# Layer 0's last two strips in a written order, the sums over A dealt anew between diffusion and sort, and X W gathered ahead of later rows of A^T

## The chip, the core and the metric

The kernel runs on one core of a Trainium2 chip. Its engines work side by side, each through its own list of instructions in order, and wait for one another by semaphores: PE (TensorE, matmuls into PSUM), DVE (VectorE), ACT (ScalarE), POOL (GpSimd) and SP (SyncE, which here only issues DMAs). POOL and ACT issue DMAs too. The metric is the device time of one execution in microseconds (us); lower is better.

## What is computed

Two layers over a graph of N = 2708 nodes with D = 128 features. `adj` is a 0/1 matrix; in the text A is `adj`, and A^T its transpose, which the kernel is also given. Cut to what matters, the reference is:

```python
# layer 0
deg = clip(adj.sum(axis=1), 1.0); dis = deg ** -0.5
diffusion = dis[:, None] * adj * dis[None, :] @ x - x
attn = softmax(beta * sim * adj, axis=1)            # sim: cosines of the rows of x
x = layernorm(x + diffusion + sigmoid(alpha) * (attn @ x - x))
# layer 1
XW = x @ W
s_col, s_row = XW @ a[0, :f], XW @ a[0, f:]
den = exp(leaky_relu(s_row[:, None] + s_col[None, :], 0.01))
num = A @ den
H = A @ (where(num != 0, den / num, 0) @ XW)
out = layernorm(x + H)
```

`den` has one of two forms for a pair of nodes, according to the sign of `s_row + s_col`. The kernel uses that: it sorts the nodes k by `s_row` and the nodes j by `s_col` into NG = 24 groups of at most 126, and gets `num` for one group of columns j from the one before by adding the rows of A^T whose k changes sides. So `num` needs one matmul of 128 rows per group and strip instead of a full product with A.

## The kernel before

The columns of A^T are cut into NS = 6 strips: five of 512 and a last one of 148. The rows are cut into NB = 22 blocks of 128. The work goes in these stages:

1. Attention of layer 0, strip after strip (to about 217 us).
2. **Diffusion** (L762 to L871 of the profile's lines). For each strip `s`, 22 matmuls (L771) add `x_sb` times the strip of A^T, which SP loads ahead (`load_strip`, L754). Then the strip is turned into rows (`to_rows`), attention is added (`h`), the layernorm's statistics are taken, `x1` is written and turned back (`x1_t`). Two matmuls give the scores of layer 1 as rows, `sb_ps`, for `s_row` (k = 1) and `s_col` (k = 0). `tally` counts on DVE how many of them lie beyond 256 thresholds, `picked` takes the same scores as a column, ACT copies `sr_b`, and `e2` is an Exp of the limited scores that POOL spreads into `e2_w`. At last X W (`xw`) is stored to HBM. Strips 0 to 4 are free for the scheduler to weave into one another; `strict` is filled at the last strip, and from there on `mm`, `dve`, `act` and `gps` keep the order in which the source writes them.
3. **Sums over A.** Group 0 starts from the sum of all rows of A^T weighted with `e2`. It is collected in `tot` by two kinds of job. An "e" (`first_strips`) loads the first 1536 columns of one row block (768 KB) into one of three `nat` buffers and adds them with 4 matmuls. A "k" (`kept_strips`) adds the row block's columns of strips 3 to 5, which are still in SBUF, with 6 matmuls. `fill("ek")` puts such jobs into PE's order at that place. Row blocks 0 to 7 (`EARLY_ROWS = 8`) are loaded by POOL and added in the diffusion, four behind strip 3 and four behind strip 4. The others are loaded by SP, each as soon as its buffer is free.
4. **Sort.** From the counts (`ct`, summed over all six strips) DVE and PE find the groups' bounds: `spread_ps`, `more` and `fits`, `reach_ps` and `can_ps`, then `ends`, a chain of eleven dependent DVE steps, `ends_ps`, `thr_ps`, `thr`. With them it numbers the nodes of k and of j (`k_gt` to `k_onp`, the same for j), and matmuls make tables of node numbers and scores (`tab_ps`, `k_sel`, `j_sel`). `k_no` and `j_no` are the node numbers by which POOL gathers rows of A^T (`gather`, into a ring of RING = 4) and rows of X W (`gather_xw`).
5. **Groups.** For each group g, `multiply` makes `num` strip by strip (three PSUM banks), DVE or ACT copies it to `q`, `carry` hands the first two rows on into the next group's ring buffer, ACT takes Ln, DVE divides, ACT takes Exp, and two groups later `weigh` adds `m_acc` from `q` and the gathered `xws`. The group's weights `wt` come from `gb`, an Exp of the group's scores; for groups 0 to 3 they are made on the spot, and for the later ones `g_r` is stored to `g_d` and read back, spread over all partitions.
6. H = A^T-blocks times `m_sb`, the last layernorm, and the output.

In stage 5 the helpers record most instructions under L176, those of stage 2 under L185, L190 and L195, so an instruction is found by its tile's name.

Of the kernel before, what the change touches and what calls it, by code (L numbers as in the profile page):

```python
# [11 lines left out]
ALU = mybir.AluOpType  # L12
# [25 lines left out]
EARLY_ROWS = 8  # L38
# [7 lines left out]
def grouped(  # L46
# [162 lines left out]
    def to_rows(acc, v, nb, ps):  # L209

        t = lp.tile([P, SW], F32, tag="to_rows", name="tr_sb", bufs=2)
        if v < nb * P:
            nc.gpsimd.memset(t[:, v : nb * P], 0.0)
        nc.scalar.copy(t[:, :v], acc[:, :v])
        rows = ps.tile([P, SW // P, P], F32, tag="tp", name="tr_ps")
        for b in range(nb):
            mm(nc.tensor.transpose, rows[:, b, :], t[:, ts(b, P)], ident)
        return rows

    def layernorm_stats(h, nb):  # L220
# [7 lines left out]
        nc.scalar.activation(rstd[:, :nb], mv[:, :nb, 1], AF.Sqrt, bias=eps)  # L228
# [61 lines left out]
    with ExitStack() as es:  # L290
# [173 lines left out]
        def attended(s, acc, total):  # L464
# [10 lines left out]
            rows = to_rows(acc, v, nb, ps_tp)  # L475
# [180 lines left out]
    def tally(s, src, lim, op, k):  # L656

        for h in range(2):
# [105 lines left out]
    for s in range(NS):  # L764
        v, nb = width(s), blocks(s)
        if 2 <= s + 1 < NS - 1:
            load_strip(s + 1)
        st = strips[s]
        acc = ps_acc.tile([P, SW], F32, tag="acc", name="dif_acc")
        for jb in range(NB):  # L770
            nc.tensor.matmul(  # L771
                acc[:, :v],
                x_sb[:, jb, :],
                st[:, jb, :v],
                start=(jb == 0),
                stop=(jb == NB - 1),
            )
        if s == 0:
            attended(*ended)
        if s == NS - 1:  # L780
            strict.append(s)
        rows = to_rows(acc, v, nb, ps_tp)

        h = work2.tile([P, SW // P, D], F32, tag="h", name="h")
        for b in range(nb):
            ib = s * 4 + b
            dve(
                "scalar_tensor_tensor", h[:, b, :], rows[:, b, :], dis[:, ib : ib + 1], att[:, ib, :],
                ALU.mult, ALU.add,
            )  # L790
        mv, rstd = layernorm_stats(h, nb)
        for b in range(nb):
# [3 lines left out]
        wide = nb * P  # L796
        if strict:
            fill("ekeke")
        tp = ps_tp.tile([P, SW // P, P], F32, tag="tp", name="x1_ps")
        for b in range(nb):  # L800
            mm(nc.tensor.transpose, tp[:, b, :], x1[:, s * 4 + b, :], ident)
        x1_t = work2.tile([P, SW], F32, tag="x1_t", name="x1_t")
        dve(
            "tensor_copy", x1_t[:, :wide], tp[:, :nb, :].rearrange("p b i -> p (b i)")
        )
        if strict:
            fill("e")

        cols = slice(s * SW, s * SW + wide)
        pbs = []  # L810
        for k, lim, op in ((1, ntheta, ALU.is_ge), (0, theta, ALU.is_le)):
            pb = ps_mm.tile([P, SW], F32, tag="mm", name="sb_ps")
            mm(
                nc.tensor.matmul, pb[:, :wide], wa_bc[:, k, :], x1_t[:, :wide],
                start=True, stop=True,
            )
            tally(s, pb, lim, op, k)
            pbs.append(pb)
        if strict:

            dve("tensor_reduce", ct, cnt.rearrange("p s k h -> p (k h) s"), AX.X, ALU.add)
            fill("ek")
            ct_ps = spread_out(ct, 4)
            far = small.tile([P, 2], F32, tag="far", name="far")
            dve("tensor_scalar", far, ct[:, 2:4], G + 0.5, None, ALU.add)
            fill("ek")
        nc.scalar.activation(sr_b[:, cols], pbs[0][:, :wide], AF.Copy, scale=1.0 - LEAK)
        for pb, dst in zip(pbs, (sr_p, sc_p)):
            for b in range(nb):
                ib = s * 4 + b  # L830
                junk = work2.tile([P, P], F32, tag="picked", name="picked", bufs=2)
                dve(
                    "scalar_tensor_tensor", junk, pb[:, ts(b, P)], 1.0, ident, ALU.mult,
                    ALU.mult, accum_out=dst[:, ib : ib + 1],
                )
        mine = slice(s * 4, s * 4 + nb)
        dve("tensor_scalar", low[:, mine], sr_p[:, mine], LIMIT, -LIMIT, ALU.min, ALU.max)
        if s == NS - 1:
            mine = slice((s - 1) * 4, s * 4 + nb)
        if s != NS - 2:  # L840
            nc.scalar.activation(e2_p[:, mine], low[:, mine], AF.Exp, scale=LEAK)
            nc.gpsimd.tensor_copy(e2_w[:, mine, 1], e2_p[:, mine])
        if strict:
            reach_ps, can = reached(ct_ps)
        pn = ps_mm.tile([P, SW // P, D], F32, tag="mm", name="xw_ps")
        for b in range(nb):
# [4 lines left out]
        xw = (nat if strict else work2).tile(  # L851
            [P, 2 if strict else 4, D], F32, tag="xw_last" if strict else "xw", name="xw",
            bufs=1 if strict else 2,
        )
        if strict:
            act(
                "activation", reach_b[64:], can[64:], AF.Copy, scale=-1.0,
                bias=Q + 1.0,
            )
            dve("tensor_copy", reach_b[:64], reach_ps[:64, :Q])  # L860
# [962 lines left out]
```

## Time and profile before

| | us |
|---|---|
| three runs | 750.27, 749.93, 749.05 (median 749.93) |
| the profiled execution | 753.27 |
| its span, first to last instruction | 751.5 |
| PE busy | 717.0 (95%) |
| DVE, ACT, POOL busy | 444.8, 418.6, 232.1 |
| mean granted PE clock | 0.972 |

| stretch of the span | us | PE busy | DVE busy | ACT busy | PE clock | DMA share |
|---|---|---|---|---|---|---|
| 336.0 to 347.9 | 11.90 | 10.21 | 4.92 | 0.90 | 1.00 | 0.74 |
| 347.9 to 361.0 | 13.10 | 9.95 | 7.92 | 2.45 | 0.90 | 0.76 |
| 361.0 to 375.5 | 14.50 | 11.07 | 8.48 | 0.76 | 0.85 | 0.87 |
| 375.5 to 388.0 | 12.50 | 9.35 | 10.47 | 8.25 | 0.73 | 0.41 |
| 435.6 to 444.5 | 8.90 | 8.90 | 8.19 | 6.71 | 1.00 | 0.76 |

A line of the timeline gives the start, the length, the engine, the source line, the operation, the tile written and the tile read, how many records were merged (a matmul in f32 leaves two records), and in brackets how long the engine had been idle and whose work it had waited for. The clock is the share of full TensorE speed that was granted.

### The profile page before, as it was taken

The page shows a single profiled execution, that of the slowest core. Times are in us where ns is not written, and L with a number is a line of the kernel's source. Part 1 is how long each engine was busy: PE and PEld are TensorE (multiplying, and loading weights), DVE is VectorE, ACT ScalarE, POOL GpSimd, SP SyncE. Part 2 cuts the span into 40 slices and gives each one's busy share as a digit, 9 for nine tenths or more (in the row PEclk, how much of TensorE's full clock was granted, in tenths as well). Part 3 has the DMA queues.
Part 4 walks back from the last instruction along what each step waited for, and adds up shares of the span by engine and source line. Part 5 has one row for each costly group of instructions (what it writes and reads, how often), then busy time and mean ns, then how long its engine had stood idle before and what let it go on. Part 6 is the DMA issues. An engine that isn't in the chain of part 4 may idle for free. (4 is left out here: it accounts for less than half of the span.)

```text
span 751.5 us, 7960 instructions
## 1 busy us (share of the span) xinstructions
PE 717.0 (95%) x2639; PEld 361.8 (48%) x2639; DVE 444.8 (59%) x927; ACT 418.6 (56%) x600; POOL 232.1 (31%) x239
## 2 busy tenths in 40 slices
PE   8999999999999999998789699999999999999995
PEld 5454444555564444445456244444444446444444
DVE  5677857576442345335585789999899993103032
ACT  4757777788741212110165889999999995001000
POOL 5867688879770000100003232222222300000000
PEclk9999999999989999999868899999999999999998
DMA  8868999989899999417837974444444531999970
GB/s 288 292 228 299 310 323 341 341 305 314 279 391 390 374 333 321 169 32 245 304 94 233 217 212 158 152 152 154 162 170 171 171 116 52 302 297 314 318 227 23
DMA packets 67524, 179.89 MB, mean 239 GB/s; under 512 B 4239, under 2 KB 18355, under 8 KB 64451
## 3 DMA queue, kind: packets, MB, share of 16 engines
q1 hardware_dynamic: 55012, 134.11, 52.0%
q0 software_dynamic: 6192, 42.29, 17.5%
q10 hardware_dynamic: 6270, 2.90, 1.3%
q8 instruction: 23, 0.38, 0.2%
q14 instruction: 27, 0.21, 0.1%
HBM read 176.44 MB, written 2.84 MB: 239 GB/s over the span
## 5 line engine op out<-in xcount | busy, mean ns | idle before, releaser
L201 POOL TENSOR_TENSOR total<-total,p_t 128x512 f32<-128x512 f32 (+3 forms) x111 | 125.4, 1131 | 36.1 <-ACT p_t L195 30.4
L176 PE MATMUL m_acc<-q,xws 128*128 128x512 f32 x240 | 123.0, 600 | 3.0 <-ACT q L176 3.0
L771 PE MATMUL dif_acc<-strip,x_sb 128*128 128x512 f32 (+1 forms) x264 | 104.0, 543 | 0.0
L176 PE MATMUL num<-ring,wt 128*128 128x512 f32 x216 | 98.4, 548 | 3.4 <-DVE q L176 1.8
L190 DVE SCALAR_TENSOR_TENSOR p_t<-sim,gentle,piece 128x512 f32<-128x512 f32 (+1 forms) x111 | 72.1, 670 | 48.2 <-PE sim L185 38.1
L185 PE MATMUL att_acc<-p_t,x_sb 128*128 128x512 f32 (+1 forms) x228 | 96.5, 549 | 2.5 <-ACT p_t L195 2.3
L176 DVE COPY q<-num 128x512 f32<-128x512 f32 (+1 forms) x141 | 83.9, 613 | 11.5 <-PE num L176 11.1
L176 DVE SCALAR_TENSOR_TENSOR q<-sr_b,nc_s,q 128x1536 f32<-128x1536 f32 (+1 forms) x48 | 77.8, 1623 | 16.1 <-ACT q L176 16.1
L195 ACT ACTIVATE p_t<-p_t,shift 128x512 f32<-128x512 f32 (+1 forms) x111 | 68.9, 654 | 30.9 <-DVE p_t L190 27.1
L176 PEld LDWEIGHTS m_acc<-q,xws 128*128 128x128 f32 x240 | 45.9, 192 | 60.3 <-issue 56.3
L1360 PE MATMUL h_acc<-ring,m_sb 128*128 128x512 f32 x164 | 72.3, 593 | 0.0
L176 ACT ACTIVATE q<-q,head,rest 128x1536 f32<-128x1536 f32 (+1 forms) x48 | 70.3, 1508 | 1.9 <-DVE ring L176 1.6
L771 PEld LDWEIGHTS dif_acc<-strip,x_sb 128*128 128x128 f32 x264 | 46.4, 190 | 48.4 <-issue 48.1
L176 ACT ACT_TABLE_LOAD x50 | 64.2, 1283 | 3.8 <-issue 2.9
L176 ACT ACTIVATE q<-q,c_s 128x1536 f32<-128x1536 f32 (+1 forms) x48 | 62.9, 1355 | 3.3 <-DVE q L176 3.0
L176 ACT ACTIVATE row<-row 128x1354 f32<-128x1354 f32 x44 | 58.2, 1323 | 11.0 <-DMA row<-in_adj 11.0
L176 PEld LDWEIGHTS num<-ring,wt 128*128 128x128 f32 x216 | 39.4, 192 | 48.4 <-issue 34.4
L185 PEld LDWEIGHTS att_acc<-p_t,x_sb 128*128 128x128 f32 x228 | 40.1, 198 | 45.4 <-ACT p_t L195 25.3
L1370 ACT COPY ht<-h_acc 128x512 f32<-128x512 f32 (+1 forms) x6 | 3.2, 535 | 91.6 <-PE h_acc L1360 91.5
L1375 DVE TENSOR_TENSOR hh<-rows,x 128x512 f32<-128x512 f32 (+1 forms) x6 | 3.8, 641 | 84.4 <-PE rows L1294 82.0
L176 POOL DMA_INDIRECT ring<-in_adj_t,k_no x18 | 19.5, 1082 | 107.9 <-PE num L176 100.3
L1360 PEld LDWEIGHTS h_acc<-ring,m_sb 128*128 128x128 f32 x164 | 30.8, 190 | 36.8 <-issue 36.8
(282 smaller groups left out, 910.9 us busy)
## 6 DMA issues: line engine op xcount, KB each, us to landing
row<-in_adj SPq DMA_DIRECT2D x44, 677.0 KB, 5.5
strip<-in_adj_t SPq DMA_DIRECT2D x10, 2816.0 KB, 15.6
piece<-in_adj_t SPq DMA_DIRECT2D x24, 1024.0 KB, 7.1
ring<-in_adj_t SPq DMA_DIRECT2D x20, 1024.0 KB, 5.1
nat<-in_adj_t SPq DMA_DIRECT2D x14, 768.0 KB, 6.3
x_sb<-in_adj_t SPq DMA_DIRECT2D x7, 1024.0 KB, 5.6
nat<-in_adj_t POOLq DMA_DIRECT2D x8, 768.0 KB, 6.3
piece<-in_adj_t SPq DMA_DIRECT2D x7, 512.0 KB, 7.5
```

The lines of the kernel that those rows point to most:

```text
L176: latest[engine] = op(*args, **kwargs)
L185: op(*args, **kwargs)
L190: return getattr(nc.vector, op)(*args, **kwargs)
L195: return getattr(nc.scalar, op)(*args, **kwargs)
L201: getattr(nc.gpsimd, op)(*args, **kwargs)
L771: nc.tensor.matmul(acc[:, :v], x_sb[:, jb, :], st[:, jb, :v], start=(jb == 0), stop=(jb == NB - 1),)
L1360: nc.tensor.matmul(acc[:, : h1 - h0], m_sb[:, kb + b, :], a[:, b, h0:h1], start=(kb + b == 0), stop=(kb + b == NB - 1),)
L1370: nc.scalar.copy(ht[:, h0:h1], acc[:, : h1 - h0])
L1375: nc.vector.tensor_tensor(hh[:, b0 : b0 + n, :], rows[:, :n, :], x1[:, ib + b0 : ib + b0 + n, :], ALU.add)
```

## The change

- `EARLY_ROWS` goes from 8 to 9. The early rows of A are issued after strips 1, 2 and 3, three each, and not after strips 3 and 4, four each.
- The loop body of the diffusion is cut into functions, and the loop runs over strips 0 to 3 only. Strips 4 (`s`) and 5 (`t`) are written out below it in one order, with `strict` filled right after the diffusion matmuls of strip 4. Those of strip 5 are dealt out in three parts (blocks 0 to 3, 4 to 17, 18 to 21) between the steps of strip 4.
- Score banks of strip 5 come from other PSUM pools. `picked` of strips 4 and 5 moves behind the counts, as does the Exp of `e2`, and X W of both strips is stored by one DMA.
- The `fill` jobs are dealt anew: fewer ahead of `ends_ps`, one between `ends_ps` and `thr_ps`, more behind `thr_ps`, fewer at the tables of j.
- In the sort, `valued_by_dve("j", 0, ...)` moves behind `rows_of_table("k", ...)`, twelve instead of five values of j are made ahead of the copy of the second table of k, and DVE instead of ACT copies `j_t[:, 0]`.
- The gathers go in the order `gather(1)`, `gather_xw(0)`, `gather(2)`, `gather_xw(1)`, `gather(3)`; before, `gather(1)` to `gather(3)` came ahead of both of `gather_xw`.
- The copies out of `tot` (`carry_in`) are split anew between ACT and DVE, two of them on ACT.
- The weights of groups 1 to 3 and `g_r` move from ahead of the first group to behind its second strip (`later_weights`, with one PSUM bank `c_ps`), and the read of `g_d` is cut in two DMAs, groups 4 to 7 first.
- `helped`, the copies of `num` that ACT makes, loses (1, 0), which DVE makes now.

```diff
-EARLY_ROWS = 8
+EARLY_ROWS = 9
...
+    for s in range(NS - 2):
+        v, nb = width(s), blocks(s)
+        if s > 0:
+            load_strip(s + 1)
+        acc = ps_acc.tile([P, SW], F32, tag="acc", name="dif_acc")
+        diffuse(s, acc)
...
+        for kb in {1: (0, 1, 2), 2: (3, 4, 5), 3: (6, 7, 8)}.get(s, ()):
+            first_strips(kb, nc.gpsimd)
...
+    s, t = NS - 2, NS - 1
+    acc = ps_acc.tile([P, SW], F32, tag="acc", name="dif_acc")
+    diffuse(s, acc)
+    strict.append("end of the diffusion")
+    acc_t = ps_acc.tile([P, SW], F32, tag="acc", name="dif_acc")
+    diffuse(t, acc_t, 0, 4)
+    h_s = mixed(s, turned(to_sbuf(acc, SW, 4), 4, ps_tp))
+    diffuse(t, acc_t, 4, 18)
+    mv_s = moments(h_s, 4)
+    to_x1(s, h_s, *mv_s)
+    tp = x1_turned(s)
+    diffuse(t, acc_t, 18, NB)
+    x1_s = x1_in_sbuf(s, tp)
+    row_s = scores(s, x1_s, 1, score_bank())
+    rows = turned(to_sbuf(acc_t, width(t), blocks(t)), blocks(t), ps_tp)
+    col_s = scores(s, x1_s, 0, score_bank())
+    tally(s, row_s, 1, (0,))
+    h_t = mixed(t, rows)
+    mv_t = moments(h_t, blocks(t))
+    shared_row(s, row_s)
+    fill("eke")
+    tally(s, row_s, 1, (1,))
+    to_x1(t, h_t, *mv_t)
+    tp = x1_turned(t)
+    tally(s, col_s, 0, (0,))
+    x1_t = x1_in_sbuf(t, tp)
+    fill("k")
+    row_t = scores(t, x1_t, 1, ps_tp.tile([P, SW], F32, tag="tp", name="sb_ps"))
+    col_t = scores(t, x1_t, 0, ps_acc.tile([P, SW], F32, tag="acc", name="sb_ps"))
+    tally(s, col_s, 0, (1,))
+    tally(t, row_t, 1)
+    tally(t, col_t, 0)
+
+    dve("tensor_reduce", ct, cnt.rearrange("p s k h -> p (k h) s"), AX.X, ALU.add)
+    fill("ek")
+    ct_ps = spread_out(ct, 4)
...
+    shared_row(t, row_t)
+    picked(t, col_t, sc_p)
+    picked(t, row_t, sr_p)
+    picked(s, row_s, sr_p)
+    fill("ek")
+    reach_ps, can = reached(ct_ps)
+    limited(s * 4, NB)
+    picked(s, col_s, sc_p)
+    act("activation", reach_b[64:], can[64:], AF.Copy, scale=-1.0, bias=Q + 1.0)
+    dve("tensor_copy", reach_b[:64], reach_ps[:64, :Q])
+    e2(s * 4, NB)
...
+    store_xw(s, xw, 6)
+    fill("ekekek")
...
+    fill("k")
     for h in range(2):
         hit = tmp.tile([P, NG - 1], F32, tag=f"hit{h}", name="hit")
...
-    fill("ekk")
+    fill("ekekk")
...
-    fill("ekekkk")
+    fill("kekekekek")
     j_gt = beyond("j", vj)
...
-    k_tab = table("k", k_onp, 0, *banks("x"), P - G, lambda: fill("e"))
+    k_tab = table("k", k_onp, 0, *banks("x"), P - G, lambda: fill("kk"))
     valued("k", 1, k_hot, low, 17)
+    valued("j", 1, j_hot, cs_p, 0, 12)
     j_run, j_ahead, j_of = numbered("j", j_hot)
+    k_no = rows_of_table("k", k_tab, G)
+    valued_by_dve("j", 0, j_hot, from_n)
+    k_tab = table("k", k_onp, 1, *banks("x"), 0, lambda: fill("kkk"))
+    valued("j", 1, j_hot, cs_p, 12)
     fill("k")
-    valued_by_dve("j", 0, j_hot, from_n)
-    k_no = rows_of_table("k", k_tab, G)
-    valued("j", 1, j_hot, cs_p, 0, 5)
-    k_tab = table("k", k_onp, 1, *banks("x"), 0, lambda: fill("kkk"))
-    valued("j", 1, j_hot, cs_p, 5)
-    fill("kkkk")
...
-    for g in range(1, RING):
-        gather(g)
+    gather(1)
...
+    dve("tensor_copy", j_t[:, 0, :], j_of_value[1])
...
+    weights(0, gb[:, 0, :])
+    j_tab = selected("j", j_t, [0, 1])
+    carry_in(0, (2, 3), by_dve)
...
+    j_no = rows_of_table("j", j_tab, P)
...
+    carry_in(1, (0, 1), by_act)
+    carry_in(1, (2, 3), by_dve)
...
-    for g in range(2):
-        gather_xw(g)
+    gather_xw(0)
+    gather(2)
+    gather_xw(1)
+    gather(3)
+
+    def later_weights():
+
+        o = ps_num.tile([P, SW], F32, tag="num", name="c_ps")
+        for g in range(1, 4):
+            spread_c(o[:, ts(g - 1, P)], g)
...
+        act("activation", g_r[:NG], o[:NG, 3 * P :], AF.Exp)
+        nc.sync.dma_start(g_d, g_r[:NG, P - G :])
...
+        for g in range(1, 4):
+            weights(g, gb[:, g, :])
+        for g0, g1 in ((4, 8), (8, NG)):
+            nc.sync.dma_start(
+                wt[:, g0:g1, P - G :],
+                g_d[g0:g1, :].unsqueeze(0).to_broadcast([P, g1 - g0, G]),
+            )
...
-    helped = {(0, 1), (0, 3), (1, 0)}
+    helped = {(0, 1), (0, 3)}
...
                 multiply(g, *item)
+                if (g, s) == (0, 1):
+                    later_weights()
```

`diffuse`, `to_sbuf`, `turned`, `mixed`, `moments`, `to_x1`, `x1_turned`, `x1_in_sbuf`, `scores`, `picked`, `shared_row`, `limited`, `e2` and `store_xw` hold the instructions of the old loop body. `moments` ends with ACT's square root, and `to_x1` begins with the reciprocal. `spread_c(o, g)` is the one matmul that lays the scores of group g over all partitions.

## The prediction

> **What bounds the kernel now.** I read the page's row of slices first, then windows by stage, then each engine in order of time between 336 and 445 us. All times below are us into the profiled span of the kernel before.
>
> ```profile
> PE   8999999999999999998789699999999999999995
> PEclk9999999999989999999868899999999999999998
> ```
>
> ```profile
> 388.00:405.90 17.90, 16.59 (x301) 13.71 (x301) 13.07 (x23) 10.60 (x45) 5.12 (x5) 0.81 0.43 148
> 405.90:435.60 29.70, 23.33 (x46) 9.75 (x47) 18.94 (x23) 22.74 (x23) 5.90 (x6) 0.83 1.01 222
> 444.50:640.00 195.50, 194.82 (x532) 93.40 (x531) 169.34 (x211) 184.87 (x169) 40.94 (x38) 1.00 0.43 148
> ```
>
> The columns are length, busy time of PE, PEld, DVE, ACT and POOL, then granted clock, DMA share and GB/s. From 444.5 on PE is busy 194.82 of 195.50 us: what starts earlier ends earlier by as much. The change acts ahead of that, where PE has holes and half clock. The holes, engine by engine:
>
> ```profile
> 357.23 0.20 DVE L176 TENSOR_REDUCE ct<-cnt 128x4 f32<-128x24 f32 x1
> 358.62 1.51 PE L176 MATMUL tot<-nat,e_w 128*32 128x384 f32 x8 [2.28 <-DMA nat<-in_adj_t]
> 361.03 1.53 PE L176 MATMUL spread_ps<-ident,ct 128*128 128x128 f32 x8
> 373.14 1.51 PE L176 MATMUL tot<-nat,e_w 128*32 128x384 f32 x8 [3.43 <-DMA nat<-in_adj_t]
> 375.56 0.62 PE L176 MATMUL ends_ps<-both,ones 128*128 128x23 f32 x2
> 388.03 1.53 PE L176 MATMUL tab_ps<-k_onp,k_ons 128*32 128x128 f32 x42 [2.49 <-DVE k_onp L176]
> 405.88 6.51 PE L176 MATMUL num<-x_sb,wt 128*128 128x512 f32 x12 [0.24 <-ACT gb L176]
> 425.11 2.05 PE L176 MATMUL m_acc<-q,xws 128*128 128x512 f32 x2 [3.00 <-ACT q L176]
> ```
>
> The chain is DVE's: counts `ct`, bounds, thresholds, places. Twice its next PE step (`spread_ps`, `ends_ps`) stands in PE's queue behind a sum over a row of A^T (an "e") that is still landing: `ct` is ready at 357.4, `spread_ps` runs at 361.03; `both` ends at 372.2, `ends_ps` runs at 375.56. That is 3.6 + 3.3 us.
>
> The last line names ACT, but ACT's power of that `q` had ended at 420.5. The DMA view, asked for the one issue at 405.14, gives the real releaser:
>
> ```profile
> xws<-xw_d,j_no POOLq DMA_INDIRECT x1, 19.8
> ```
>
> 405.14 + 19.8 = 424.9. The three gathers of A^T ahead of it on POOL's queue (400.19, 401.59, 402.95) landed after 9.4, 14.7 and 21.0 us: one queue, one behind the other.
>
> **The change, part by part.**
>
> *Sums inside the diffusion.* Nine e rows instead of eight, three each in strips 2, 3, 4 (before: 0-3 in strip 4's, 4-7 in strip 5's). Three rows cost PE 0.80 + 2.05 = 2.85 us (332.90 to 333.70 and 334.29 to 336.34). A strip without rows takes 22.7 (two tr_ps, 260.94 and 283.60). Strip 4's diffusion so ends at 260.1 + 3 x 22.7 + 3 x 2.85 = 336.8, not 332.9: 3.9 later. Against it, PE's 1.69 us wait for row 7 at 341.32 goes, and rows 9-11 can load from SP as soon as 6-8 are summed (about 314), long before their use at 346.
>
> The rule that speaks against this: the Trainium skill, "DMA: Bandwidth & Descriptors", Issuing engines are not separate DMA queues, says that DMAs of all issuers share the same 16 engines and interleave. POOL's rows 3-8 now fly beside the loads of strips 3 and 4, which landed 12.5 and 13.4 us after issue without such company. By the rule strip and three rows (5.77 + 2.36 MB at the 372 GB/s of 240 to 264) finish after 21.9 us; the strip is wanted 25.5 us after issue. Both give a loss of 0, the rule with a margin of 3.6.
>
> *Last two strips in written order.* From 336.8: four blocks of strip 5 (0.275 each) hide ACT's copy, tr_ps 337.9, `h` 338.6 to 339.7, four stats pairs in strict order (0.41 each, as at 352.06) to 341.35, rstd, x1 to 343.04; 14 blocks of strip 5 hide that, x_ps to 343.25, last four blocks to 344.35. Scores of strip 4 then; DVE: tally 345.4, `h` and stats of strip 5 to 347.4. The second tally waits for ACT's read of the same bank, which is queued behind rstd: 348.4, a new wait of 1.0. x1 to 349.75, tally, x1_t to 350.84, tally, four short tallies (0.293 each) from 351.6: `ct` at 352.9 instead of 357.23, **4.3 earlier**.
>
> *From ct to the k tables.* `spread_ps` at 353.1, no DMA ahead of it (row 11 is there). Eight of the twelve `picked` (0.21 each) now stand before `more`: 354.9, and `fits` end at 356.85. ACT writes reach_b at 357.9 (1.02 behind, as before) and only then loads the Exp table (1.28) for e2; before, that load lay in a wait at 357.11. DVE's `back` needs e2 and stands ahead of `ends`: 359.9 instead of 358.05, a new loss of 1.85. `ends` to `both` takes 6.5: `ends_ps` at 366.45 instead of 375.56, 9.1 earlier. One k between (1.1 at half clock) costs 0.2: `thr` 368.8 instead of 377.73. `k_of` ends 3.5 on, 372.3, and DVE has j_gt until 373.1.
>
> PE has "ekekk" before `ahead`, and it sat idle from about 362.4 to 366.4. Row: after the 3.43 us hole at 373.14 the clock stayed at 0.50 until 382, and e and k took 1.28 and 1.09 instead of 0.66. Five would end at 374.4, k_run at 375.0. Rule (the Trainium skill, "TensorE: Matmul & The Clock Gate", Part 1: The HAM clock gate): full clock returns after about 3.4 us of busy PE; then k_run waits for DVE alone, 373.1. The nearest row is the restart at 358.62, sums back to back as here: clock 1.00 from 362 on, 3.4 us later. I take half clock to 371: `ahead` at 372.9, k_run 373.5 instead of 381.94. k_onp takes the same 6.1: 379.6.
>
> Then "kekekekek" (5 k, 4 e). With three buffers row 21 is issued when row 18 is summed, 374.5. Such loads landed after 4.2 and 6.1 (issues at 341 and 352). At 5.0: 379.5, and e and k behind it end at 380.8, later than DVE. **k tables at 380.8 instead of 388.03: 7.2 earlier** (bounds: 379.6 and 383).
>
> *From the k tables to the first group (T = 380.8).* PE has been busy, so its clock should be full here, where before it read 0.50. k_no T+2.9 (was 3.6), then valued_by_dve (1.08), which before lay in the wait for k_no: j_run T+4.1, j_onp T+6.95 to T+10.1 (was T+10.95), j tables to T+11.35 (was T+14.4, because "kkkk" held PE). Twelve values of j now stand on ACT ahead of the copy of k table 1 (T+6.0, was T+7.8), where nothing waits. gb exp and weights(0) end 1.32 after the tables, T+12.7. Before, the first `num` came 2.2 us behind weights(0), since its bank waited for ACT's exps of groups 1 to 3; those are moved into group 0. gather(0) is issued at T+3.4 and took 7.0: hidden. **First num at 393.5 instead of 405.88; 5.2 of it here.**
>
> *First groups.* Moving the exps and three weights behind `num` (0,1) holds ACT's copy of (0,3) and delays the first Ln by 1.1 (S+8.4 from the first num S; was S+7.33). Dropping ACT's copy (1,0), which waited behind Ln and held PE 1.54, gives that back. X W of group 0 is issued at T+13.3 behind one gather alone and lands near S+6; `m_acc` wants it at S+16.4. Its cost: ring2 and ring3 are issued later, land near S+11 and S+18, wanted at S+15.5 and S+24. The half of weights' DMA for groups 4-7 comes first and is wanted at S+29. With PE no longer held at 425.11 nor cold to 430, what ends last is DVE's copies: step 3 starts at S+24.4 instead of S+29.76 (435.64). **5.3 earlier.**
>
> Sum: 7.2 + 5.2 + 5.3 = 17.7; I take 17, as some hand-overs have no row. The profiled execution took 753.27 (span 751.5); it would take about 736.3. The runs shown have a median of 749.93, 3.3 lower, so **732.9**.
>
> **Rivals.**
> B, the carry chain sets the start of the groups: each group's first two rows come from the one before through PE, DVE and back. If DVE, not X W, was last there, 5.3 goes: gain 12.4, 737.5. For it: DVE busy 18.94 of 29.70, ring copies between. Against: PE stood still at 425.11 after DVE had caught up at 423.1.
> C, PE becomes the bound before the k tables: half clock throughout and late rows put T at 386, and cold j tables take 2 more: gain about 8, 741.9. For it: clock 0.73 to 0.85 in those stages. Against: e and k fill DVE's time, and DVE was 10.47 of 12.50 busy.
> D, slower: the three-buffer ring. Rows 12, 15, 18, 21 each start when the row three before is summed, a loop of landing + 0.7. With landing L: row 21 at 347 + 4L + 2. At L = 4 to 6.3 it hides. At L = 12.1 (the longest seen) row 21 lands at 397.4, T is 398.7, 10.7 late, which eats the 10.5 gained behind it; from L = 12.1 on it decides, and L = 13 gives 753.7. Against: the 12.1 is one of 22 loads, median 6.3.
> That the written order isn't there is excluded: the built program's order shows it.
>
> **How the numbers follow.** A (as worked, 12.5 to 21.1) 0.66, B 0.15, C 0.12, D 0.05, other 0.02. A measurement tells 0.2%, 1.5 us. Best end: row 21 in time (1.2), k_run at 373.1 (0.4), the first two `num` at full clock (1.75): 21.1, 728.8. High end: C, 741.5. Faster 0.92, same 0.02, slower 0.06.
>
> **What would show it.** `ct` near 353, `spread_ps` directly behind it, `ends_ps` near 366, k tables near 381, first `num` near 393.5, no wait of `m_acc` 0 in group 2, PE full from about 410. Wrong if e rows 12 to 21 still wait for DMA, if the half clock covers 366 to 396, or if ring2 or ring3 lands late.

## The result, and the profile after

| | before | after |
|---|---|---|
| runs, median (lowest to highest) | 748.80 us (744.82 to 753.98, 20 runs) | **742.07 us** (736.38 to 748.73, 20 runs) |
| the profiled execution: time, span, mean granted clock | 753.27, 751.5, 0.972 | 739.68, 737.9, 0.982 |

The ratio is 0.9897, with a 95% interval of 0.9873 to 0.9920: 7.7 us faster (6.0 to 9.5). This ratio, like every ratio, interval and mean below, leaves out the runs that lie more than 1.5% above the fastest of their kernel (here the one of 748.73), which the medians and ranges contain. Forecast were 17 us, 732.9, with a range up to 741.5. The two profiled executions, set side by side, differ by 13.6 us, nearly twice as much as the runs. That gap between the pair of profiles and the runs is what the experiments had to explain.

First the profile after: its rows of PE's busy share and clock, then its windows from `ct` to the k tables, to the first `num`, to step 4, and the steady groups (columns: length, busy time of PE, PEld, DVE, ACT and POOL, clock, DMA share, GB/s).

```profile
PE   7999999999999999999798899999999999999995
PEclk9999999999979999999989999999999999999999
```

```profile
353.10:380.90 27.80, 22.57 (x285) 15.47 (x280) 22.27 (x79) 11.99 (x44) 0.93 (x5) 0.88 0.73 247
380.90:395.30 14.40, 12.49 (x267) 11.13 (x258) 10.25 (x17) 8.76 (x36) 3.76 (x2) 0.88 0.53 182
395.30:429.30 34.00, 30.68 (x76) 13.89 (x77) 29.33 (x40) 28.51 (x30) 12.63 (x10) 0.95 0.95 222
429.30:640.00 210.70, 208.92 (x568) 100.19 (x567) 170.98 (x224) 186.77 (x171) 41.79 (x38) 1.00 0.49 162
```

The stretch from the k tables to the first `num` has shrunk from 17.9 to 14.4 us, and PE is as full in the steady groups as it was (208.92 of 210.70). In time order, PE and DVE of the same trace:

```profile
353.13 0.20 DVE L176 TENSOR_REDUCE ct<-cnt 128x4 f32<-128x24 f32 x1
360.00 0.18 DVE L176 TENSOR_TENSOR back<-live,e_p 128x22 f32<-128x22 f32 x1 [1.52 <-ACT e_p L176]
366.65 0.59 PE L176 MATMUL ends_ps<-both,ones 128*128 128x23 f32 x2 [3.71 <-DVE both L176]
379.73 0.85 PE L176 MATMUL tot<-nat,e_w 128*32 128x384 f32 x8 [0.97 <-DMA nat<-in_adj_t]
380.89 1.38 PE L176 MATMUL tab_ps<-k_onp,k_ons 128*32 128x128 f32 x42
389.54 4.48 PE L176 MATMUL tab_ps<-j_onp,j_ons 128*32 128x128 f32 x88 [1.59 <-DVE j_onp L176]
395.32 1.99 PE L176 MATMUL num<-x_sb,wt 128*128 128x512 f32 x4 [0.29 <-ACT wt L176]
411.25 1.92 PE L176 MATMUL m_acc<-q,xws 128*128 128x512 f32 x2
```

`ct`, `ends_ps` and the k tables stand where the prediction had them (352.9, 366.45, 380.8). PE no longer waits for a row of A^T ahead of `ends_ps`, but for DVE, and the first `m_acc` waits for nothing. Two things are not as forecast. The tables of j take 4.48 us, not the 3.00 that they take at full clock (in after_again, below), and `m_acc` takes 1.92 for two halves and not 1.02: both run in part at half clock. What released `m_acc` is read in the DMA view, asked for the one issue at 396.02:

```profile
xws<-xw_d,j_no POOLq DMA_INDIRECT x1, 2.6
```

X W lands 2.6 us after issue, where it took 19.8 in the first trace of before.

### The profile page after: what moved, and what is told of

It reads as the page before. It is cut to its first block, busy times and chain, and to the rows that moved or that the text cites. A ratio compares the mean times of both kernels' runs of the same rounds, so it can differ in the third digit from the quotient of the medians.

```text
span 737.9 us, 7958 instructions
## 1 busy us (share of the span) xinstructions
PE 708.7 (96%) x2639; PEld 358.8 (49%) x2639; DVE 443.8 (60%) x925; ACT 419.5 (57%) x601; POOL 233.9 (32%) x240
## 3 DMA queue, kind: packets, MB, share of 16 engines
q0 software_dynamic: 6336, 43.08, 17.7%
## 5 line engine op out<-in xcount | busy, mean ns | idle before, releaser
L201 POOL TENSOR_TENSOR total<-total,p_t 128x512 f32<-128x512 f32 (+3 forms) x111 | 124.5, 1122 | 38.3 <-ACT p_t L195 32.8
L185 PE MATMUL dif_acc<-strip,x_sb 128*128 128x512 f32 x220 | 98.4, 594 | 0.0
L185 PEld LDWEIGHTS dif_acc<-strip,x_sb 128*128 128x128 f32 x220 | 40.5, 190 | 45.8 <-issue 45.8
L176 POOL DMA_INDIRECT ring<-in_adj_t,k_no x18 | 21.1, 1170 | 100.3 <-PE num L176 97.2
L1451 PEld LDWEIGHTS h_acc<-ring,m_sb 128*128 128x128 f32 x164 | 30.8, 190 | 36.8 <-issue 36.8
```

The lines of the kernel that those rows point to most:

```text
L176: latest[engine] = op(*args, **kwargs)
L185: op(*args, **kwargs)
L201: getattr(nc.gpsimd, op)(*args, **kwargs)
L1451: nc.tensor.matmul(acc[:, : h1 - h0], m_sb[:, kb + b, :], a[:, b, h0:h1], start=(kb + b == 0), stop=(kb + b == NB - 1),)
```

## The experiments

Every row of the table below is one traced execution. All but before_third and after_third, which are that one execution alone, were also timed beside the kernel before on the same chip; the chips differ from one group of runs to another. Five times are read from each trace: `ct`, the first k table, the first `num`, and the first `num` of step 4 (which reads x_sb again). "To end" is from there to the end of the span. "Lost" is the sum of (1 - granted clock) over slices of 1 us from `ct` to 448.

The theories, by the letters that the expectations use. 1, later sharpened to H: the one traced execution of before was unusual, long at half clock, and much of what the prediction summed isn't there in others. 2: the difference lies in transfers. 3: a wait that the change added (for e2) eats gain. Q: X W, behind three gathers of A^T, sets when the old groups go on, so that an earlier front gains nothing by itself. R: the other edits of the changed rear lose time in the first groups. N: a measurement of few runs was lucky.

| trace | start to ct | to k tables | to first num | to step 4 | to end | lost |
|---|---|---|---|---|---|---|
| before, first | 357.2 | 30.8 | 17.9 | 38.6 | 307.0 | 15.3 |
| before_again | 358.7 | 27.3 | 18.1 | 31.2 | 310.3 | 3.4 |
| before_third | 358.5 | 27.5 | 14.6 | 36.8 | 309.0 | 8.5 |
| after, first | 353.1 | 27.8 | 14.4 | 34.0 | 308.6 | 6.8 |
| after_again | 354.4 | 28.5 | 12.9 | 34.9 | 308.2 | 5.1 |
| after_third | 353.1 | 28.0 | 14.4 | 34.0 | 306.7 | 6.8 |
| after_fourth | 352.4 | 26.9 | 14.4 | 34.0 | 306.7 | 5.1 |
| front_only | 354.4 | 26.8 | 16.1 | 38.3 | 309.6 | 6.9 |
| rear_only | 356.9 | 29.1 | 13.1 | 34.9 | 307.6 | 8.5 |
| gathers_as_before | 354.7 | 29.3 | 14.6 | 36.9 | 306.7 | 6.8 |
| before_xw_ahead | 358.1 | 28.3 | 16.3 | 32.9 | 307.1 | 8.5 |
| before_xw_second | 356.4 | 29.2 | 18.4 | 32.8 | 307.0 | 10.2 |
| front_xw_ahead | 353.5 | 27.9 | 14.2 | 34.8 | 310.7 | 6.8 |
| front_xw_second | 356.0 | 28.3 | 14.3 | 31.2 | 306.8 | 3.4 |
| front_xw_back | 351.7 | 26.6 | 14.3 | 31.2 | 309.1 | 3.4 |
| back | 356.8 | 25.5 | 12.9 | 34.0 | 309.4 | 3.4 |
| back_and_groups | 355.1 | 24.9 | 14.4 | 32.3 | 308.8 | 3.4 |
| warm | 354.1 | 28.9 | 14.6 | 32.3 | 309.4 | 3.4 |
| copy_back_on_act | 354.1 | 27.5 | 12.9 | 34.1 | 309.3 | 3.4 |
| weights_first | 351.3 | 27.7 | 13.6 | 33.8 | 306.6 | 6.8 |

### Was the first trace of before a usual execution?

Both kernels were run again, unchanged.

*before_again*

> The kernel before, unchanged, profiled in another execution. Theory 1 (the base of the sum was an unusual execution): its profiled execution was 4.5 us above the median of its runs because PE stood at half clock for longer; this one has a span near 747 and a mean clock above the 0.972 of the first, and the stages that differ are those at half clock (370 to 380 and 420 to 430). Theory 2 (the runs without a recorded trace are faster for another reason, the transfers): clock 0.972 again, and the difference lies in waits for DMA.

Measured: 748.21 us in the median of 22 runs (743.10 to 753.85), as in the first measurement, and its profiled execution has a span of 745.6 at a clock of 0.982. Its windows from `ct` on:

```profile
358.70:386.00 27.30, 20.39 (x244) 13.62 (x244) 20.21 (x63) 10.38 (x40) 0.99 (x5) 0.87 0.74 264
386.00:404.10 18.10, 14.88 (x300) 11.58 (x300) 13.03 (x23) 10.59 (x44) 5.11 (x5) 1.00 0.60 194
404.10:435.30 31.20, 27.83 (x68) 12.44 (x69) 26.57 (x33) 26.01 (x27) 8.09 (x8) 1.00 0.97 237
```

```profile
418.48 1.02 PE L176 MATMUL m_acc<-q,xws 128*128 128x512 f32 x2
```

The clock is 1.00 behind the k tables, where it read 0.81 and 0.87 in the first trace. And the wait of 3.00 us at the first `m_acc`, on which the prediction's last step rests, isn't there: X W was issued at 403.36 and landed 12.1 later. Theory 1 holds for this trace; how usual the wait is, two traces cannot say.

*before_third*

> The kernel before, a third execution. Theory H: from ct to the k tables about 27 to 28 and no wait of m_acc for X W, as in the second trace. Theory Q: from ct to the k tables anywhere from 27 to 31, and m_acc waits 2 to 3 us for X W or lies within 2 us of it.

```profile
418.62 2.04 PE L176 MATMUL m_acc<-q,xws 128*128 128x512 f32 x2 [3.47 <-DMA xws<-xw_d,j_no]
```

Measured: 748.12, and the wait is there again, 3.47 us, with half clock behind it (2.04 for what takes 1.02). So the wait for X W is common (theory Q), while the 30.8 us from `ct` to the k tables are not: 27.3 and 27.5 in the other two (theory H). The first trace of before had both, and lost 6.8 us of clock more than the third.

*after_again, after_third, after_fourth*

> The changed kernel, unchanged, profiled in another execution. Its 20 runs lie at 736 to 740 and at 741 to 745. Theory 1: the two groups differ by PE's half clock; a span near 741 comes with a mean clock near 0.977, and the 4 to 5 us more lie in one or two spells of half clock on the path (layer 0 at 200 to 214, the tables of j at 388 to 394, the first groups at 410 to 414). Theory 2: clock 0.982 as in the first trace, and the difference lies in waits for rows of A^T or for X W.

> The changed kernel, a third execution. Both theories: ct near 354, k tables near 382, first num near 395.5, no wait of m_acc, 34 to 35 us from the first num to step 4 with one spell of half clock at 410 to 414.

> The changed kernel beside the three others, on the same chip: ratio 0.987 to 0.990, as in its first two measurements.

Measured: 740.03 (6 runs, ratio 0.9872, 0.9817 to 0.9928), 737.90 (one run), and 740.31 (21 runs, ratio 0.9915, 0.9890 to 0.9940, a little above the 0.987 to 0.990 expected). The four traces agree within 2 us in each stage. The longest of these runs is not in a trace, so theory 1's account of the scatter between 736 and 745 was not seen directly. Over the runs that list a clock, time falls with clock (correlation -0.64 in 53 runs of before, -0.73 in 24 of after; 0.01 of clock goes with 4 and 6 us): a relation, not yet a cause.

### Filling PE's holes, and the wait for e2

*warm*

```diff
+    busy(ends_ps, 8)
     mm(nc.tensor.matmul, ends_ps[:, : NG - 1], ones, both, start=True, stop=True)
...
+    busy(j_of_value[1], 3)
...
             if g < NG:
+                busy(accs[4], {(1, 4): 3, (1, 5): 2, (2, 0): 2}.get((g, s), 0))
                 multiply(g, *item)
```

`busy(t, n)` is n multiplications of ones, 256 columns wide.

> The changed kernel with multiplications of ones in three of PE's holes (8 ahead of ends_ps, 3 ahead of the tables of j, 7 ahead of three num of groups 1 and 2), written to unused columns. Theory 1: full clock from 366 on, tables of j 1.9 us shorter (4.5 to 2.6), the first m_acc no longer at half clock (1.5 us): 3.4 us faster than the changed kernel, 738.7 against 742.1, and less scatter. Theory 2 (the holes are what counts, not the clock): no faster, or 1 us slower by the added work.

Measured: 740.58 (6 runs), ratio 0.9880 (0.9828 to 0.9931): level with the changed kernel, as theory 2 has it. The trace shows what became of the clock, PE first, then windows:

```profile
363.89 3.72 PE L176 MATMUL ends_ps<-ones 128*128 128x256 f32 x16
...
380.78 1.51 PE L176 MATMUL tot<-nat,e_w 128*32 128x384 f32 x8 [2.05 <-DMA nat<-in_adj_t]
```

```profile
363.80:379.00 15.20, 12.97 (x167) 9.35 (x160) 13.57 (x31) 7.77 (x33) 0.00 (x0) 1.00 0.89 313
379.00:387.00 8.00, 6.22 (x88) 4.68 (x88) 2.25 (x4) 2.62 (x13) 0.00 (x0) 0.57 0.04 14
```

With the hole filled the clock stays at 1.00 until 379. PE then runs through its sums faster, stands before row 21 of A^T for 2.05 us instead of 0.97, and is cold from there to 387, on the k tables. In this trace the half clock, taken away in one place, came back behind the next wait. In the groups it did go: 32.3 instead of 34.0 to step 4.

*back*

```diff
-    back = tab.tile([P, NB], F32, name="back")
-    dve("tensor_tensor", back, live, e2_p, ALU.mult)
...
     k_onp = placed("k", k_own)
+    back = tab.tile([P, NB], F32, name="back")
+    dve("tensor_tensor", back, live, e2_p, ALU.mult)
```

> The changed kernel with the product live x e2 (back) taken out of DVE's way ahead of the chain of ends and put behind k_onp. Theory 3 (the wait for e2, 1.5 us in the trace, is on the path to the k tables): ends_ps 1.5 us earlier, and 0.6 to 1.5 us faster in all. Rival: row 21 of A^T ends last ahead of the k tables, so that ends_ps comes 1.5 earlier and the end 0.5 us or less.

```profile
368.68 0.37 PE L176 MATMUL ends_ps<-both,ones 128*128 128x23 f32 x2 [2.03 <-DVE both L176]
```

Measured: `ct` at 356.84 in this trace, so 11.84 us from `ct` to `ends_ps`, where the changed kernel's first trace has 13.52: 1.7 less, as worked. The k tables come 25.5 after `ct` instead of 26.9 to 28.5. The time is 739.80 (14 runs), ratio 0.9891 (0.9856 to 0.9926): a gain of 1 or 2 us is in the trace and below what the runs can tell.

*back_and_groups* puts this and six of the multiplications of the groups together.

> The changed kernel with back behind k_onp, and six multiplications of ones ahead of three num of groups 1 and 2. Theory H: the half clock at 410 to 414, which is in all three traces of the changed kernel, goes and gives 1.3 us; back gives the 2.2 to 2.7 us between ct and the end that its trace showed: 737 against the changed kernel's 740 to 742. Rival: row 21 and DVE's copies of q end last anyway, and it is within 1 us of the changed kernel.

Measured: 740.29 (16 runs), ratio 0.9893 (0.9859 to 0.9926), though its one trace has a span of 735.4 and 24.9 and 32.3 in the two stages. The runs don't bear out the 3 us that the trace shows.

### The change in halves

*front_only* is the changed kernel up to the numbering of the rows (`numbered("k", ...)`) with the old text behind it; *rear_only* is the reverse. The orders of the sums were closed up so that each row is summed once.

> The changed kernel up to the numbering of the rows, the kernel before from there on (tables of j, gathers, first groups). The prediction's steps: k tables 7.2 us earlier and nothing else, 740.5 against 747.8. Theory H (half clock and what it makes late was large in the one execution that the sum was made against; most of the time behind ct isn't there to be gained): ct about 4.5 us earlier, from ct to the k tables 27 to 28.5 as in the second trace of before, from there to the first num 18, on to step 4 31 to 34: 743.3.

> The kernel before up to the numbering of the rows, the changed kernel from there on. The prediction's steps: 5.2 (k tables to first num) and 5.3 (first groups), 737.3 against 747.8. Theory H: 13 to 14.4 instead of 18 from the k tables to the first num, but 34 instead of 31.2 from there to step 4: 3 us faster, about 745.

Measured: front_only 747.66 (14 runs), ratio 0.9985 (0.9959 to 1.0011), 1.1 us or nothing, where 740.5 and 743.3 were expected: both theories miss. rear_only 743.36 (21 runs), ratio 0.9922 (0.9896 to 0.9948), 5.8 us, with 13.1 and 34.9 in the two stages, as theory H has them; the prediction's steps gave 737.3. The front does what was forecast in its own stage, k tables at 381.19; the gain is lost behind it. PE and the windows of front_only:

```profile
416.47 2.04 PE L176 MATMUL m_acc<-q,xws 128*128 128x512 f32 x2 [3.19 <-DMA xws<-xw_d,j_no]
```

```profile
384.00:396.00 12.00, 9.20 (x192) 7.25 (x193) 9.85 (x17) 7.76 (x32) 4.98 (x4) 1.00 0.71 209
396.00:408.00 12.00, 10.21 (x27) 4.67 (x27) 6.23 (x11) 7.84 (x12) 4.45 (x4) 0.86 1.01 221
408.00:420.00 12.00, 6.98 (x12) 2.60 (x13) 7.99 (x10) 11.05 (x9) 2.21 (x2) 0.75 1.00 204
```

The first `num` runs at 397.24, 3.4 us earlier than in before_third, and the first `m_acc` only 2.2 earlier (416.47 against 418.62). The DMA engines are full from 396 on (share 1.00) and move 204 to 221 GB/s; X W, issued at 396.5 behind three gathers of A^T, takes 19.8 us. In the traces with the old order of gathers the first `m_acc` runs at 416 to 419 (once 425), whenever the first `num` ran.

Something else comes with that order. In three of its five traces (before_again, front_only, gathers_as_before) the tables of j, made while the three gathers fly, take 5.8, 4.6 and 4.4 us at full clock instead of 2.8 to 3.0. PE has short holes in them for which the profile names no releaser, here one in before_again:

```profile
397.47 0.43 PE L176 MATMUL tab_ps<-j_onp,j_ons 128*32 128x128 f32 x5 [0.42 <-issue]
```

What causes them is open. They are in the 18.1 us of before_again and in the 16.1 of front_only.

*gathers_as_before*

```diff
-    gather(1)
+    for g in range(1, RING):
+        gather(g)
     wt = ring_p.tile([P, NG, P], F32, name="wt")
...
     gather_xw(0)
-    gather(2)
     gather_xw(1)
-    gather(3)
```

> The changed kernel with the gathers of A^T 1, 2 and 3 issued together ahead of X W, as before. The prediction's step: X W of group 0 lands behind three gathers and holds PE; 3 to 5 us slower than the changed kernel, 744 to 747. Theory H: X W is issued near 396 and lands 12 us later, 408, ahead of its use at 411; no wait of m_acc, and the time within 1 us of the changed kernel's 740 to 742.

```profile
416.06 2.05 PE L176 MATMUL m_acc<-q,xws 128*128 128x512 f32 x2 [1.77 <-DMA xws<-xw_d,j_no]
```

Measured: 743.11 (14 runs), ratio 0.9915 (0.9883 to 0.9948), and the wait is back. The trace takes 36.9 to step 4 instead of 34.0 to 34.9. Both expectations miss: theory H left the wait out, and the prediction's step is of the right kind, but the means give 1.6 us (742.0 to 740.4, with an interval that reaches 0) where it has 5.3.

### The gathers alone, and with the front

*before_xw_ahead, before_xw_second*: one edit in the kernel before, the reverse of the last diff (`gather(1)` alone ahead, then X W of 0, row 2, X W of 1, row 3). *front_xw_ahead, front_xw_second*: the same edit in front_only.

> The kernel before with nothing changed but the order of the gathers: X W of groups 0 and 1 issued ahead of rows 2 and 3 of A^T. The prediction's step: 5.3 us faster, 743. Theory H (the first trace of before was an unusual execution): m_acc waits for X W in some executions only, so 1 us or less, 747 to 748. Theory Q (the gathers set when the first groups can go on, in most executions): no wait of m_acc, from the first num to step 4 31 to 32, and 2 to 3 us faster, 745 to 746.

> The kernel before with X W ahead, again. Theory Q (X W is what holds the old groups): ratio 0.988 to 0.992, 6 to 9 us. Theory N: its six runs were lucky, and the gain is the 3 to 5 us that the traces show (m_acc's wait of 3.0 to 3.5 us and the half clock behind it), ratio 0.993 to 0.996.

> The changed kernel up to the numbering, the kernel before from there on, but with X W of groups 0 and 1 ahead of rows 2 and 3 of A^T. Theory Q (what the front gains is taken back by X W, which lands no earlier when the first num does): no wait of m_acc, the first num near 397, step 4 near 429 to 430, and 4 to 6 us faster than the front alone, 742 to 744. Theory H (the front gains little in the runs even where nothing waits): 746 to 747.

> The changed front with the old rear and X W ahead, again, beside the changed kernel. Theory R (the changed rear loses in the first groups: from the first num to step 4 it takes 34 to 35, the old rear with X W ahead 31.4 and whatever it waits for rows of A^T): 4 to 6 us faster than the changed kernel, ratio to before 0.982. Theory N (the five runs were lucky): level with the changed kernel within 2 us, ratio 0.988 to 0.990.

Measured: before_xw 741.65 (6 runs), ratio 0.9884 (0.9852 to 0.9916), then 743.67 (22 runs), ratio 0.9961 (0.9934 to 0.9988). front_xw 737.18 (5 runs), ratio 0.9823 (0.9798 to 0.9849), then 737.58 (12 runs), ratio 0.9885 (0.9851 to 0.9919). As theory N has it, the repeats gain less; for front_xw the difference lies mostly in the runs of before beside it (749.4, then 746.8 in the mean). Repeats fall outside each other's intervals, so the scatter from one measurement to the next is larger than an interval says, and I go by the mean over all these measurements (95%: 1.96 standard errors):

| mean, us | old front | changed front |
|---|---|---|
| gathers as before | 748.0 +- 0.4 (163 runs) | 747.6 +- 0.8 (14 runs) |
| X W ahead | 743.6 +- 1.2 (28 runs) | 738.2 +- 1.1 (17 runs) |
| the whole changed rear | 743.4 +- 1.4 (rear_only, 18 runs) | **740.4 +- 0.8** (after, 45 runs) |

The front is worth 0.4 us with the gathers as before and 5.4 with X W ahead: the two parts of the change need each other. The other parts of the rear add nothing to X W ahead with the old front, and lose some 2 us (738.2 to 740.4) with the changed one, so that front_xw is quicker than both kernels compared here (side by side on one chip, 738.3 +- 1.1 in 12 runs against 740.2 +- 1.1 in 20). Where transfers hold the front's gain even so is seen in one of the two traces of front_xw, at step 4:

```profile
430.35 1.10 PE L176 MATMUL num<-x_sb,wt 128*128 128x512 f32 x2 [3.41 <-DMA x_sb<-in_adj_t,k_no]
```

In the other trace that row was there in time, and the stage took 31.2 us at full clock:

```profile
398.60:429.80 31.20, 27.83 (x68) 12.44 (x69) 26.57 (x33) 29.09 (x30) 12.91 (x10) 1.00 0.96 239
```

*front_xw_back* adds the edit of back.

> The same with back behind k_onp. The wait for e2 (1.5 us) is on the path to the k tables: ends_ps 1.5 us earlier, k tables 1 to 2 earlier; if rows of A^T then hold the groups (3.4 us at step 4 in the first trace), 0 to 1 us faster than without, ratio 0.981 to 0.983.

Measured: 738.75 (6 runs), ratio 0.9898 (0.9840 to 0.9955); its trace has a span of 732.9, with 26.6 and 31.2. The runs don't tell it from front_xw, and the ratio of 0.981 to 0.983 expected is missed.

### What the changed rear loses

*copy_back_on_act* and *weights_first* undo one edit each in the changed kernel.

```diff
-    helped = {(0, 1), (0, 3)}
+    helped = {(0, 1), (0, 3), (1, 0)}
```

```diff
+    later_weights()
     for step in range(NG + LAG):
...
-                if (g, s) == (0, 1):
-                    later_weights()
```

> The changed kernel with the copy of num (1,0) on ACT again. If DVE's copies of q set the first groups (three waits of PE for them, 3.3 us in the traces): from the first num to step 4 1 to 2 us less, 32 to 33. The prediction's step: the copy waits behind the first Ln on ACT and holds PE, 1.1 to 1.5 us more, 35 to 36.

> The changed kernel with the weights of groups 1 to 3 ahead of the first num again. If their place costs the first groups time: from the first num to step 4 32 to 33 and the first num 1 us later (c_ps, 1.2 us, now ahead of it), the sum unchanged or 1 us less. The prediction's step: the first num comes 2 us later and the first Ln 1.1 earlier, 1 us slower in all.

Measured: 738.86 (4 runs, ratio 0.9846, 0.9776 to 0.9916) with 34.1 to step 4, and 735.62 (4 runs, ratio 0.9814, 0.9741 to 0.9886) with 33.8. Both stay outside what was expected of that stage (32 to 33, or 35 to 36 with the copy on ACT).

The copy on ACT changes nothing that the traces show: the two stages take 12.9 and 34.1, and where the changed kernel's PE waits three times for DVE (1.42, 0.82 and 1.06, together 3.30 us), here it waits once for ACT and twice for DVE (1.54, 0.70 and 1.13, together 3.37). The first of these waits, in the changed kernel and with the copy on ACT:

```profile
406.33 1.13 PE L176 MATMUL num<-ring,wt 128*128 128x512 f32 x2 [1.42 <-DVE q L176]
404.80 1.98 PE L176 MATMUL num<-ring,wt 128*128 128x512 f32 x4 [1.54 <-ACT q L176]
```

With the weights first, the first `num` comes 13.6 after the k tables instead of 12.9 (the changed kernel where the tables of j keep their clock), and step 4 is reached 0.2 sooner behind it. The four runs lie 4.4 below the changed kernel's mean (736.0 against 740.4), but on a chip on which the changed kernel was not timed, and the trace is 2 us early at `ct` already, ahead of the edit. Whether this edit loses time stays open.

What the traces do show is that without the half clock the two rears would be about level. From the k tables to step 4 front_xw_second and front_xw_back take 45.5 and lose no clock; the four traces of the changed kernel take 47.8 to 48.4 and lose 1.7 to 3.4, in the tables of j and in the first groups. That is 45.0 to 46.1 without the lost clock (an estimate, since a wait can hide half clock). The spell in the first groups is in every trace of the changed rear but the two where multiplications filled the holes (warm, back_and_groups), and both traces of before_xw lose 1.6 to 1.7 there too. But the runs of warm and back_and_groups are no quicker than those of the changed kernel, so the half clock is not shown to be what the 2 us in the runs are made of, and which edit brings it stays open.

## Why the prediction was wrong

**The step that failed: the sizes of the terms behind `ct`, read from one execution of before.** The sum 7.2 + 5.2 + 5.3 was made against the one trace, whose waits and half clock were taken for the kernel's. The last paragraph took 17 from 753.27 and then lowered the result by the 3.3 us by which the runs shown were quicker, as if those 3.3 lay outside the stages that it had summed. They lay inside. That trace lost 15.3 us of full clock behind `ct`, the two others 3.4 and 8.5; it took 394.3 us from `ct` to its end, the others 386.9 and 387.9. Stage by stage, with the 7.2 divided at `ct`:

| us gained | forecast | first trace against first | means of 3 and 4 traces |
|---|---|---|---|
| start to `ct` | 4.3 | 4.1 | 4.9 |
| `ct` to the k tables | 2.9 | 3.0 | 0.8 |
| k tables to the first `num` | 5.2 | 3.4 | 2.8 |
| first `num` to step 3 | 5.3 | 4.6 | 1.3 |
| step 3 to the end | 0 | -1.5 | 1.2 |

Against the trace that it was made for, the sum reaches 15.1 of its 17.7 by step 3. Between the means the three terms behind `ct` come to 4.9 where 13.4 were forecast. Even those means give 11.0 in all and the runs 7.7, for seven traces are few. Nor is the 0 of the last row firm: from step 4 to the end the twenty traces take 306.6 to 310.7, without order by kernel.

**The sums and the written order: right.** 4.3 were forecast for `ct`; 4.1 in the pair, and 4.9 between the means (358.1 to 353.2). The last halves of strips 3 and 4, in company of rows of A, landed 24.1 and 24.0 us after issue, where the prediction's rule of shared engines gave 21.9, and PE waited for neither. (The 12.5 and 13.4 of the prediction were a first half and the median of two halves; the last half of strip 4 took 17.0 before.) The new load of the Exp table ahead of e2 cost 1.52 for the forecast 1.85, and taking it away gave 1.7 in the trace. Row 21 came 0.97 late, also as worked.

**From the k tables to the first `num`: right at full clock, which the change does not always have.** T + 12.7 was forecast for weights(0), and after_again has its first `num` at T + 12.9:

```profile
391.48 3.00 PE L176 MATMUL tab_ps<-j_onp,j_ons 128*32 128x128 f32 x88 [1.55 <-DVE j_onp L176]
```

The three other traces have T + 14.4, because the clock falls to half for 3.4 us inside the tables of j. "PE has been busy, so its clock should be full here" was the wrong sentence. PE stood 1.59 us before `j_onp`; but it stood 1.55 in after_again too, so the hole alone does not decide it. The gain comes from where the prediction put it: behind the tables of j the changed rear takes 1.3 us to the first `num`, the old one 3.4 and more in all its traces. Of these 2.1 the moved weights give 0.7 (weights_first takes 2.0), and most of the rest is the copy of `j_t` by DVE, for whose forerunner on ACT PE had waited, as in front_xw_second:

```profile
396.64 0.62 PE L176 MATMUL j_sel<-four,j_t 128*128 128x24 f32 x4 [1.04 <-ACT j_t L176]
```

Against this the tables of j begin 8.6 after the k tables and not 7.8 as with the old rear behind the changed front, which reaches its first `num` after 14.2 to 14.3 with X W ahead.

**The first groups: the wait was real, its price was not.** X W ahead takes the wait away in every trace, and that alone makes the kernel before 4.4 us faster in the runs (748.0 to 743.6), near the 5.3 of the step. But to step 3 the three traces of before take 29.8, 22.4 and 28.0 us: without the wait for X W, before_again is faster there than the forecast 24.4 and than the changed kernel's 25.2. The changed kernel has half clock at 410 to 414, where the prediction had full clock, and `c_ps` (1.16 us), which the old rear did ahead of the first `num`. "Dropping ACT's copy gives that back" is not borne out: PE's wait for ACT became one for DVE.

**Rivals.** B (12.4 us) is half right: X W did hold PE beyond DVE in the old order (3.0 and 3.5 us in two traces of three), but with X W in time DVE's copies are what ends last (the 3.30 us of waits above). C put PE's half clock ahead of the k tables; the half clock it named was there, 366 to 373, but the k tables came at 380.89, near the 380.8 of the sum and not at 386. Its cold tables of j came true in three traces of four (1.5 us of the 2). D didn't happen. No rival had the base as its subject. C's 741.9 (741.5 where the prediction gives its range) is near the right time by luck.

## What to carry to other kernels

Before a gap of one trace is priced, look for it in a second execution of the same kernel: here the largest terms were real waits, but a good part of their size belonged to that execution alone. When two parts of a change feed the same transfers, price them together: an earlier start was worth 0.4 us until the one small gather that it ran into was issued ahead of three large ones, and 5.4 after. Filling a hole to keep the clock here only moved the half clock behind the next load, so follow the next wait before counting the gain.

## What was not expected of the hardware

The half clock comes in pieces. In nearly every trace the lost clock of a stage is a multiple of 1.7 us, which is 3.4 us at half clock; and the same place has one, two or three pieces in different executions. The pieces lie on a grid: in the changed kernel's first trace the spells start at 202.2, 366.0, 389.9 and 410.4, which is 48, 7 and 6 times 3.413 us from one to the next, and in all twenty traces every start, and every end but that of the last spell, lies a whole multiple of 3.413 us from the first start. The grid lies elsewhere in the span in each execution. Windows of the changed kernel's first trace on four spells:

```profile
203.00:212.00 9.00, 9.00 (x34) 6.88 (x34) 4.27 (x12) 3.06 (x10) 3.30 (x8) 0.50 1.04 397
366.00:373.00 7.00, 6.35 (x51) 4.05 (x55) 4.48 (x15) 1.58 (x7) 0.00 (x0) 0.51 0.62 221
390.00:394.00 4.00, 4.00 (x81) 3.74 (x73) 1.52 (x5) 0.45 (x2) 0.44 (x1) 0.59 0.78 276
410.00:414.00 4.00, 4.00 (x6) 1.70 (x7) 3.74 (x5) 3.97 (x4) 1.23 (x2) 0.57 1.05 196
```

The Trainium skill ("TensorE: Matmul & The Clock Gate", Part 1: The HAM clock gate) calls the window of activity free-running, some 3.4 us long, and its effect variable from run to run. The grid and the counts above agree, and this is the sentence that the prediction should have used: it warns against pricing a spell from one execution.

The first of the four lines is the odd one. PE is busy all of the 9 us, with full clock on both sides, and still gets half. Of the 34 PE records in it 18 are products with `ident`, which turn a tile (`sim`, `tr_ps`), and 16 are multiplications 148 columns wide (`att_acc`):

```profile
204.29 2.58 PE L185 MATMUL sim<-ident,turned 20*128 20x20 f32 x8
...
209.04 2.67 PE L185 MATMUL att_acc<-p_t,x_sb 128*128 128x148 f32 x10
```

So a PE that is busy by the trace can be held at half clock. Whether the turning, the narrow width or something else is the reason was not tried. Between 190 and 260 us the lost clock was 0 to 6.8 us over all twenty traces, in code that no version changed, and `ct` moves with it: with the changed front it is 351.3 in the one trace with none lost, and 354.4 to 356.8 in the three with 6.8 (but 356.0 in one with 5.1). It may be a good part of the scatter of some 10 us in the runs of each kernel; the runs without a trace cannot show it.
